# Broadcast rows in one transfer, two gates one scan later, one write a slot earlier, in a Mamba and attention kernel

## The chip, the cores and the metric

The kernel runs on one core of a Trainium2 chip. The metric is the device time of one execution in microseconds (us). Before the change it is 8030.78 us, the median of three runs (8016.75 to 8032.62).

## The reference, cut to what matters

The input `x` is 4 images of 512 channels and 64 x 64 = 4096 positions. Layer 0 normalises it, cuts the 512 channels into 4 chunks of 128, and runs a Mamba block on each chunk; layer 1 is a linear attention with 8 heads. Both add to `x`. The change lies in the Mamba block, whose core is a scan over the positions with 16 states for each of 256 inner channels:

```python
def step(h, inp):
    dt_t, B_t, C_t, x_t = inp
    dA = jnp.exp(dt_t[:, :, None] * A)
    h = dA * h + (dt_t * x_t)[:, :, None] * B_t[:, None, :]
    y = jnp.einsum('bds,bs->bd', h, C_t)
    return (h, y)
...
y = ys.transpose(1, 0, 2) + xc * D_param
y = y * jax.nn.silu(z)                      # the gate
return jnp.einsum('bld,od->blo', y, out_proj_w)
```

`B_t` and `C_t` have one value for each position and state and are the same for all channels; `dt_t` and `u = dt_t * x_t` have one for each position and channel and are the same for all states.

## The kernel before

**Steps.** A step is one image, one tile of 512 positions and one chunk: 4 x 8 x 4 = 128 steps. A step has 256 channels x 16 states of scans over 512 positions. The 128 partitions hold 32 channels x 4 states at a time, so a scan instruction does 128 of the 4096 rows and a step has 32 scans. They are dealt to 16 slots of two scans. Slots 0 to 7 belong to the first 128 channels (e = 0), slots 8 to 15 to the second (e = 1). Two slots are a group: one set of 4 states (`q`), four scans, one tile `h` of 128 x 4 x 512. `h` has two buffers.

**What a group needs.** `dA` (ACT, L715) is the exponential of `dt` spread over the states; `bx` (POOL, L722, `drive`) is `u` times `B`, three slots ahead of its scan. VectorE does the scans (L775). After the group, VectorE multiplies three quarters of `h` with `C` from PSUM (L798, `product`, called behind the first scan of the next group), POOL the last quarter with `C` from SBUF (L790), and TensorE folds the states into `y` (`fold_states`). When a half is through, VectorE multiplies `y` with the silu of `z` (L818, `gate`), and `out_proj` uses that at slot 4 for the step before.

**The broadcast data.** All of it goes through DRAM and comes back spread over the partitions, issued by SyncE (SP in the profile):

- `b_all`, 128 x 512 for each group: 4 rows of `b_rows`, each to 32 partitions. `c_sb`, 128 x 128: the same for the last quarter of `c_rows`. `for_states` (L687) does either with four transfers, one per state. `c_tail` and `b_row` call it in every odd slot: `c_sb` for the group that starts next, `b_all` for a group three further on. `c_sb` has two buffers and `b_all` three.
- `d_all`: for each half, `dt` (v = 0) and then `u` (v = 1), spread over the states by four transfers of 256 KB each (`spread`, L633). The half e = 1 is spread in slots 0 and 1 of its own step, the half e = 0 of the next step in slots 7 and 9. `d_all` has two buffers. A first `drive` on the half e = 1 is issued in slot 5.
- `d_rows`: `dt` of the next step is written to DRAM in slot 4 and `u` in slot 8 (`to_rows`, L624). `u` is made by POOL in slot 6 (L631, `times_input`), in place over `dt`.

**Order.** The order of every engine's instructions is the order in which the code issues them: `slot` (L759) and the function `after` (L1146) that it calls at its end. SP issues one transfer after the other and waits at each for what that one needs: a free buffer, written rows, and one of eight completion semaphores that the program deals out in turn to SP's transfers, so that a transfer also waits until the one eight before it has landed.

Of the kernel before, what the change touches and what calls it, by code (L numbers as in the profile page):

```python
# [24 lines left out]
def kernel(  # L25
# [24 lines left out]
    nc = tc.nc  # L50
# [4 lines left out]
    NH = DI // P  # L55
# [3 lines left out]
    BLK = 32  # L59
    KS = P // BLK  # L60
# [563 lines left out]
    def to_rows(f, v, nm):  # L624

        d_rows = dram.tile([P, NH, T], F32, tag=f"d_rows{v}", name=f"d_rows{v}_{nm}")
        f["d_rows", v] = d_rows
        nc.sync.dma_start(d_rows, f["dt"])
# [43 lines left out]
    JJ = NJ // 2  # L672
    SLOTS = NH * NQ * JJ
    AWAY = (3, 10)

    def place(g):

        n, r = divmod(g, SLOTS)
        e, r = divmod(r, NQ * JJ)
        return n, e, *divmod(r, JJ)  # L680
# [5 lines left out]

    def for_states(dst, rows_, q):  # L687

        for k in range(KS):
            nc.sync.dma_start(  # L690
                dst[k * BLK : (k + 1) * BLK, :], rows_[q * KS + k, :].partition_broadcast(BLK)
            )

    def b_row(g):
        n, e, q, _ = place(g)
# [37 lines left out]
    def carry_over(g):  # L733

        n, e, _, _ = place(g)
        nc.gpsimd.tensor_tensor(
            carry[:, e], a_t[:, e],
            fs[n]["d_all", e][:, 0, :, 0].unsqueeze(2).to_broadcast([P, NJ, NQ]), ALU.mult,
        )
# [11 lines left out]
    def starts_half(g, last):  # L751

        return g < last and g % (SLOTS // NH) == 0 and steps[g // SLOTS][1] > 0

    def keep(g, h, copy):
        n, e, q, _ = place(g)
        copy(st[:, steps[n][2], e, q, :], h[:, :, T - 1])  # L757

    def slot(g, last, after):  # L759
        n, e, q, jj = place(g)  # L760
        if starts_half(g + DRIVE + 1, last):
            carry_over(g + DRIVE + 1)
        if g + DRIVE < last:
            drive(g + DRIVE)
        if jj == 0:
            hs[g // JJ] = wk.tile([P, NJ, T], F32, tag="h", name=f"h_{g}", bufs=2)
        else:
            if g + 1 < last:
                c_tail(g + 1)
            if g + 1 + 3 * JJ < last:  # L770
                b_row(g + 1 + 3 * JJ)
        h = hs[g // JJ]
        for i in range(2):
            j = jj * 2 + i
            nc.vector.tensor_tensor_scan(  # L775
                h[:, j, :], dAs.pop(2 * g + i), bx[:, g % RING, i, :], 0.0, ALU.mult, ALU.add,
            )
            if i == 1 and jj == JJ - 1 and g % SLOTS - 1 not in AWAY:
                keep(g, h, nc.scalar.copy)
            if 2 * g + i + LEAD < 2 * last:  # L780
                decay(2 * g + i + LEAD)
            if i == 0 and jj == 0 and g:
                product(g - 1)
                fold_states(g - 1, last)
        if starts_half(g + DRIVE, last):
            carry_decay(g + DRIVE)
        if jj == JJ - 1:
            if g % SLOTS - 1 in AWAY:
                keep(g, h, nc.gpsimd.tensor_copy)
            nc.gpsimd.tensor_tensor(  # L790
                h[:, :, CUT:], h[:, :, CUT:], bc(c_sb.pop(g // JJ), NJ), ALU.mult
            )
        after()

    def product(g):

        own = hs[g // JJ][:, :, :CUT]
        nc.vector.tensor_tensor(own, own, bc(c_all.pop(g // JJ), NJ), ALU.mult)  # L798
# [17 lines left out]
    def gate(f, n, e):  # L816
        z = f["xz"][:, 1, e, :]
        nc.vector.tensor_tensor(z, ys.pop((n, e)), z, ALU.mult)  # L818
# [224 lines left out]
    names = [f"{b}_{t}_{c}" for b, t, c in steps]  # L1043
    fs = [{} for _ in steps]
# [87 lines left out]
    with tc.manual_schedule():  # L1132
        credit, seen, mix, held[0], held_x[0] = 0.0, work["mm"], iter(()), 0, 0
        for n, (b, t, c) in enumerate(steps):
            f, nm = fs[n], names[n]
            before = fs[n - 1] if n else None
            nxt = fs[n + 1] if n + 1 < N else None
            front = step_inputs(n + 2) if n + 2 < N else iter(())
            last_mix, mix = mix, mixers(fs[n + 2], names[n + 2]) if n + 2 < N else iter(())
            if c == 0 and (t + 1 < NT or b + 1 < B):  # L1140
                add_to(ahead, tile_norm(b, t + 1) if t + 1 < NT else tile_norm(b + 1, 0))
            if c == 0 and t == 0 and b + 1 < B:
                add_to(light, input_norm(b + 1))
            assert c != 2 or not ahead
            for s in range(SLOTS):
                def after():  # L1146
                    nonlocal credit, seen
                    now[0] = n * SLOTS + s
                    for what in [w for at, w in due if at <= now[0]]:
                        what()  # L1150
                    due[:] = [d for d in due if d[0] > now[0]]
                    if s < 2:
                        next(last_mix, None)
                    if s in (0, 1):
                        spread(f, 1, s, nm)
                    if s == 1 and before is not None:
                        gate(before, n - 1, 1)
                    if s == 2 and nxt is not None:
                        time_banks(nxt, names[n + 1])
                    if s == 3 and nxt is not None:  # L1160
                        nc.scalar.preload_act_table_set("softplus")
                        time_steps(nxt, names[n + 1])
                        nc.scalar.preload_act_table_set("natural_log_exp_and_others")
                    if s == 6 and before is not None:
                        pb_, pt_, pc_ = steps[n - 1]
                        with_skip(before, xn[pb_, pt_], pc_)
                        if pc_ == NC - 1:
                            add_to(late, leave(pb_, pt_))
                    if s in (3, 5, 6, 7, 8, 9):
                        next(front, None)  # L1170
                    if s in (4, 8) and nxt is not None:
                        to_rows(nxt, int(s == 8), names[n + 1])
                    if s == 6 and nxt is not None:
                        times_input(nxt)
                    if s == 4 and before is not None:
                        pb_, pt_, pc_ = steps[n - 1]
                        out_proj(before, xn[pb_, pt_], pc_, names[n - 1])
                    if s in (7, 9) and nxt is not None:
                        spread(nxt, 0, int(s == 9), names[n + 1])
                    if s == 9:  # L1180
                        gate(f, n, 0)
                    if s == 10 and n + 2 < N:
                        silu(n + 2)
                        nc.scalar.preload_act_table_set("natural_log_exp_and_others")
                    if s >= 12:
                        next(mix, None)
                    may = [
                        what for k, what in ((0, "wide"), (1, "one ahead"), (2, "two ahead"))
                        if any(a - 2 * k <= s <= a - k for a in AWAY) or (k == 2 and s == SLOTS - 1)
                    ]  # L1190
                    if light and light[0][1] == "wait" or s in AWAY and not any(
                        q and q[0][1] == "wide" for q in (ahead, late)
                    ):
                        one(light)

                    limit[0] = 1 if 0 < s < 6 else 2
                    credit = min(credit + 3.5 - (work["mm"] - seen), 2.6)
                    busy = False
                    for queue in (ahead, late, rest):
                        kind = queue[0][1] if queue else None  # L1200
                        if queue is ahead or kind == "free" or credit > 0 or kind == "more" and not busy:
                            start = work["mm"]
                            one(queue, ANYWHERE if queue is ahead and (c, s) > (1, 4) else may)
                            credit -= work["mm"] - start
                            busy = busy or work["mm"] - start > 1
                    seen = work["mm"]

                slot(n * SLOTS + s, N * SLOTS, after)
            fs[n - 1].clear() if n else None
        product(N * SLOTS - 1)  # L1210
        fold_states(N * SLOTS - 1, N * SLOTS)
        now[0] = None
        for _, what in due:
            what()
# [59 lines left out]
```

## Time and profile before

| what | value |
|---|---|
| median of the runs | 8030.78 us |
| profiled execution, its own time | 8041.96 us |
| its span | 8040.3 us |
| mean granted TensorE clock | 0.891 |
| first to last `dA` (all 128 steps) | 118.0 to 7562.9 us |
| in 118 to 7563 us: VectorE busy | 6855.94 us |
| in 118 to 7563 us: POOL busy | 6681.71 us |
| in 118 to 7563 us: TensorE busy | 6005.43 us |
| in 118 to 7563 us: ACT busy | 5367.02 us |
| in 118 to 7563 us: mean busy share of the 16 DMA engines | 0.66 |
| transfers issued by SP | 11064, of which 4096 `b_all` and 4096 `c_sb` |

The busy times are those of one profiled execution. Idle time of an engine is put down to what ended it; where a wait has several semaphores, to the one that came last, and a semaphore that several transfers share in turn can carry the name of another one.

### The profile page before, as it was taken

The page shows a single profiled execution, that of the slowest core. Times are in us where ns is not written, and L with a number is a line of the kernel's source. Part 1 is how long each engine was busy: PE and PEld are TensorE (multiplying, and loading weights), DVE is VectorE, ACT ScalarE, POOL GpSimd, SP SyncE. Part 2 cuts the span into 40 slices and gives each one's busy share as a digit, 9 for nine tenths or more (in the row PEclk, how much of TensorE's full clock was granted, in tenths as well). Part 3 has the DMA queues.
Part 4 walks back from the last instruction along what each step waited for, and adds up shares of the span by engine and source line. Part 5 has one row for each costly group of instructions (what it writes and reads, how often), then busy time and mean ns, then how long its engine had stood idle before and what let it go on. Part 6 is the DMA issues. An engine that isn't in the chain of part 4 may idle for free.

```text
span 8040.3 us, 92566 instructions
## 1 busy us (share of the span) xinstructions
PE 6500.2 (81%) x24880; PEld 2130.3 (26%) x24880; DVE 6925.7 (86%) x6022; ACT 5501.7 (68%) x9185; POOL 6691.3 (83%) x4789
## 2 busy tenths in 40 slices
PE   5677777677788888888788888888778888888599
PEld 1111211121223222322222222322122232322144
DVE  5999999999999899989999999998989999988600
ACT  4667777777777777677777777777777777777421
POOL 3999999999898899889888889888989898888600
PEclk7788888888899999999899999999799999999699
DMA  5666666666666666676666666676666666677402
GB/s 151 165 166 161 153 150 159 156 158 160 168 163 169 149 165 158 172 189 170 167 159 171 171 153 162 157 183 186 160 156 160 157 159 155 155 187 183 113 32 89
DMA packets 829200, 1266.00 MB, mean 157 GB/s; under 512 B 183912, under 2 KB 317560, under 8 KB 816384
## 3 DMA queue, kind: packets, MB, share of 16 engines
q1 hardware_dynamic: 804736, 1222.32, 59.7%
q0 software_dynamic: 16896, 33.56, 2.4%
q10 hardware_dynamic: 7040, 4.20, 0.2%
q8 instruction: 195, 3.19, 0.2%
q14 instruction: 333, 2.73, 0.1%
HBM read 1052.78 MB, written 206.57 MB: 157 GB/s over the span
## 4 chain that ended last, share of the span: by engine, by line
DVE 35%; PE 25%; ACT 14%; DMA 10%; POOL 6%; issue 6%; SPq 4%; POOLq 0%; DVEq 0%; ACTq 0%
DVE h L775 21%; DVE h L798 10%; PE pq L124 5%; PE pc L124 5%; PE y L124 4%; ACT dA L715 4%; POOL bx L722 4%; DMA d_all<-d_rows 3%; SPq L690 3%; DMA c_sb<-c_rows 3%; PE pr L124 2%; PE po L124 2%; ACT xz L1083 2%; PE pp L124 2%; DMA xn<-in_x_dram 2%
## 5 line engine op out<-in xcount | busy, mean ns | idle before, releaser
L722 POOL TENSOR_TENSOR bx<-d_all,b_all 128x1024 f32<-128x1024 f32 x2048 | 4861.7, 2376 | 404.5 <-DMA c_sb<-c_rows 162.4
L775 DVE TENSOR_TENSOR_SCAN h<-dA,bx 128x512 f32<-128x512 f32 x4096 | 4753.6, 1206 | 502.8 <-ACT dA L715 236.5
L715 ACT ACTIVATE dA<-d_all,a_t 128x512 f32<-128x512 f32 x4096 | 2778.5, 686 | 1445.5 <-DVE h L775 1382.9
L798 DVE TENSOR_TENSOR h<-h,c_all 128x1536 f32<-128x1536 f32 x1024 | 1769.5, 1728 | 0.1
L790 POOL TENSOR_TENSOR h<-h,c_sb 128x512 f32<-128x512 f32 x1024 | 1317.2, 1286 | 237.2 <-ACT st L757 130.4
L124 PE MATMUL y<-h,fold 128*32 128x512 f32 x8192 | 1281.1, 702 | 138.0 <-POOL h L790 132.7
L124 PE MATMUL c_all<-parts,sel 128*128 128x384 bf16 x1024 | 369.5, 361 | 1125.8 <-DVE h L798 1123.4
L124 PE MATMUL pc<-xn,w_cv 128*128 128x512 f32 x2048 | 1042.0, 643 | 98.5 <-DVE xn L414 48.4
L124 PE MATMUL pq<-w_qk,xa 128*128 128x512 f32 x2048 | 965.8, 605 | 1.6 <-ACT xa L367 1.6
L124 PEld LDWEIGHTS <-sel 128*128 128x128 bf16 x1280 | 126.7, 99 | 1763.9 <-DVE h L798 1546.1
L124 PEld LDWEIGHTS pc<-xn,w_cv 128*128 128x128 f32 x2048 | 388.5, 200 | 721.1 <-issue 426.3
L124 PEld LDWEIGHTS pq<-w_qk,xa 128*128 128x128 f32 x2048 | 398.4, 196 | 435.2 <-issue 418.0
L124 PE MATMUL pr<-xb,m 128*128 128x512 f32 x1024 | 485.7, 613 | 4.1 <-ACT res L1014 3.2
L124 PE MATMUL pp<-xn,w_pr 128*128 128x512 f32 x1024 | 478.9, 598 | 4.8 <-DVE xn L414 4.8
L124 PEld LDWEIGHTS y<-h,fold 128*32 128x32 f32 x8192 | 171.0, 114 | 715.2 <-issue 340.8
L124 PE MATMUL y<-xz,dg 32*32 32x512 f32 x2048 | 338.7, 737 | 0.0
L124 PE MATMUL pd<-xz,w_xp 128*128 128x512 f32 x512 | 325.5, 769 | 7.8 <-ACT xz L1083 7.8
L631 POOL TENSOR_TENSOR dt<-dt,xz 128x1024 f32<-128x1024 f32 x128 | 302.0, 2360 | 31.8 <-DMA d_rows<-dt 27.5
L867 ACT ACTIVATE kq<-pq 128x512 f32<-128x512 f32 x256 | 150.6, 588 | 258.2 <-PE pq L124 257.0
L757 ACT COPY st<-h 128x4 f32<-128x4 f32 x896 | 172.4, 192 | 204.0 <-DVE h L775 201.0
L124 PE MATMUL pz<-xn,w_z 128*128 128x512 f32 x512 | 294.6, 671 | 5.4 <-ACT xz L608 5.2
L874 DVE TENSOR_TENSOR kq<-pk,kq 128x256 f32<-128x256 f32 x124 | 50.7, 409 | 250.9 <-PE pk L124 250.9
(182 smaller groups left out, 6200.0 us busy)
## 6 DMA issues: line engine op xcount, KB each, us to landing
d_all<-d_rows SPq DMA_DIRECT2D x2048, 256.0 KB, 5.1
b_all<-b_rows SPq DMA_DIRECT2D x4096, 64.0 KB, 2.2
d_rows<-dt SPq DMA_DIRECT2D x256, 512.0 KB, 6.2
c_sb<-c_rows SPq DMA_DIRECT2D x4096, 16.0 KB, 4.4
xs<-in_x_dram SPq DMA_DIRECT2D x32, 1024.0 KB, 6.7
xn<-in_x_dram SPq DMA_DIRECT2D x32, 1024.0 KB, 8.5
xr<-in_x_dram POOLq DMA_DIRECT2D x32, 1024.0 KB, 10.8
x<-xr SPq DMA_DIRECT2D x32, 1024.0 KB, 4.1
```

What stands on the lines that cost most here:

```text
L124: nc.tensor.matmul(out_, lhsT, rhs, **how)
L631: nc.gpsimd.tensor_tensor(f["dt"], f["dt"], f["xz"][:, 0], ALU.mult)
L690: nc.sync.dma_start(dst[k * BLK : (k + 1) * BLK, :], rows_[q * KS + k, :].partition_broadcast(BLK))
L715: nc.scalar.activation(dAs[k], fs[n]["d_all", e][:, 0, j, :], AF.Exp, scale=a_t[:, e, j, q : q + 1])
L722: nc.gpsimd.tensor_tensor(bx[:, g % RING], fs[n]["d_all", e][:, 1, jj * 2 : jj * 2 + 2, :], bc(b_all[g // JJ], 2), ALU.mult,)
L757: copy(st[:, steps[n][2], e, q, :], h[:, :, T - 1])
L775: nc.vector.tensor_tensor_scan(h[:, j, :], dAs.pop(2 * g + i), bx[:, g % RING, i, :], 0.0, ALU.mult, ALU.add,)
L790: nc.gpsimd.tensor_tensor(h[:, :, CUT:], h[:, :, CUT:], bc(c_sb.pop(g // JJ), NJ), ALU.mult)
L798: nc.vector.tensor_tensor(own, own, bc(c_all.pop(g // JJ), NJ), ALU.mult)
L867: nc.scalar.activation(qk[i], pq, AF.Relu)
L874: nc.vector.tensor_tensor(kq, pk, kq, ALU.add)
L1083: nc.scalar.activation(fs[n]["xz"], fs[n]["xz"], AF.Silu)
```

## The change

`for_states` issues one transfer instead of four: the source is walked as 4 rows x 32 repeats x the row, the destination as 128 partitions. The two gates move from the end of slots 1 and 9 to behind the first scan of slots 2 and 10, ahead of `product`. `u` is written out at slot 7 instead of 8, ahead of the `spread` of that slot.

```diff
     def for_states(dst, rows_, q):
-        for k in range(KS):
-            nc.sync.dma_start(
-                dst[k * BLK : (k + 1) * BLK, :], rows_[q * KS + k, :].partition_broadcast(BLK)
-            )
+        src = rows_[q * KS : (q + 1) * KS, :].unsqueeze(1).to_broadcast([KS, BLK, dst.shape[-1]])
+        nc.sync.dma_start(dst, src)
...
             if i == 0 and jj == 0 and g:
+                if g % SLOTS == JJ and n:
+                    gate(fs[n - 1], n - 1, 1)
+                if g % SLOTS == SLOTS // NH + JJ:
+                    gate(fs[n], n, 0)
                 product(g - 1)
                 fold_states(g - 1, last)
...
-                    if s == 1 and before is not None:
-                        gate(before, n - 1, 1)
...
-                    if s in (4, 8) and nxt is not None:
-                        to_rows(nxt, int(s == 8), names[n + 1])
+                    if s in (4, 7) and nxt is not None:
+                        to_rows(nxt, int(s == 7), names[n + 1])
...
-                    if s == 9:
-                        gate(f, n, 0)
```

## Prediction

> **What bounds the kernel now.** I read the engines' busy time, the waits of POOL, VectorE and SP, one step in the timeline, and then the DMA lines.
>
> ```profile
> PE 6500.2 (81%) x24880; PEld 2130.3 (26%) x24880; DVE 6925.7 (86%) x6022; ACT 5501.7 (68%) x9185; POOL 6691.3 (83%) x4789
> ```
>
> The 128 steps run from 118 to 7563 us, 58.2 us each (3.64 per slot). In that stretch VectorE is busy 92% and POOL 90%: two engines bound it together, and only their idle time can be won.
>
> ```profile
> DVE h L775 <- ACT dA L715: 236.5, 210, 3.9
> DVE h L775 <- PE y L124: 73.5, 81, 3.0
> DVE xz L818 <- PE y L124: 69.7, 82, 4.4
> DVE h L775 <- POOL bx L731: 58.0, 63, 5.3
> DVE h L775 <- POOL bx L722: 55.6, 12, 46.6
> ...
> POOL bx L722 <- DMA c_sb<-c_rows: 162.4, 115, 4.2
> POOL h L790 <- ACT st L757: 130.4, 104, 5.5
> POOL bx L722 <- DVE h L775: 91.1, 90, 4.0
> POOL bx L722 <- DMA b_all<-b_rows: 73.9, 48, 4.3
> ...
> SPq L690 <- DMA d_all<-d_rows: 1108.5, 1355, 3.4
> ```
>
> Columns: total us, times, longest. `bx` does not read `c_sb`: 115 waits in 128 steps are one per step, and the timeline shows which.
>
> ```profile
> 3982.15 1.75 SPq L690 DMA_DIRECT2D c_sb<-c_rows  x4
> 3984.01 2.59 SPq L690 DMA_DIRECT2D b_all<-b_rows  x4
> 3986.69 2.64 SPq L639 DMA_DIRECT2D d_all<-d_rows  x4
> 3989.80 3.17 SPq L690 DMA_DIRECT2D c_sb<-c_rows  x4
> 3994.33 3.67 SPq L690 DMA_DIRECT2D b_all<-b_rows  x4
> 3998.05 1.84 SPq L639 DMA_DIRECT2D d_all<-d_rows  x4
> ...
> 3999.84 2.36 POOL L722 TENSOR_TENSOR bx<-d_all,b_all 128x1024 f32<-128x1024 f32 x1
> 4005.90 2.36 POOL L722 TENSOR_TENSOR bx<-d_all,b_all 128x1024 f32<-128x1024 f32 x1 [3.70 <-DMA c_sb<-c_rows]
> ```
>
> This is slots 15, 0 and 1 on SP. The last POOL line is the first `drive` of the half e = 1: it waits for the `u` part of `d_all`, which SP could issue only at 3998.05, 8.25 us after the `c_sb` of slot 1, because each of the eight transfers before it waited for the one eight ahead to land. So SP's issue and its eight semaphores make POOL late. All POOL waits on DMA in the steps come to 348.7 us: `bx` 162.4 + 73.9 + 18.1 + 16.6 + 8.2, L790 47.0 + 16.8 + 5.7. VectorE's waits laid to POOL, straight or through `y`, are 73.5 + 69.7 + 58.0 + 9.0 (55.6 less one of 46.6 at the start) = 210.2. POOL's idle time before L722 and L790 is 404.5 + 237.2, so one us of POOL's idle time costs VectorE 210.2/641.7 = 0.33 us; were the DMA waits alone to blame, 0.6. I take 0.33.
>
> **One transfer for four rows: SP.** A step has 32 `b_all` and 32 `c_sb` transfers of 0.365 and 0.419 us (medians of the tile views), 25.1 us of SP's 58.2; 8 of each remain, 6.3 us, or 9.5 at the 0.595 us of the longest-issuing SP transfers (L295). Eight semaphores then reach back across two slots, not one.
>
> **The same: DMA engines.** What may be lost lies here. Every SP transfer of before ran on 16 engines: q1's 804736 packets are 627712 data rows plus 16 for each of 11064 transfers.
>
> ```profile
> q1 hardware_dynamic: 804736, 1222.32, 59.7%
> q0 software_dynamic: 16896, 33.56, 2.4%
> q10 hardware_dynamic: 7040, 4.20, 0.2%
> ```
>
> On q10 the rows of ACT's 27 transfers make 6680, and the other 360 are 21 x 16 + 2 x 8 + 4 x 2, where two transfers have 8 rows (`w_dt`) and four have 2 (`b_qk`). So the number of engines went with the outer count. The changed source walks 4 rows outermost against 128 partitions: the bounds are 16 engines and 4. I take 4, the row of the 2- and 8-row transfers being nearest.
>
> The Trainium skill speaks against this change: "DMA: Bandwidth & Descriptors", "Why a DMA increments its semaphore by 16 and not by 1", says the largest number up to 16 that divides the outer counts of both sides is used, here 4, and its "Rules for kernel authors" warn of a small outer dimension. By the rule the sum is the four-engine one; without it, the 16-engine rival.
>
> Mean packet times from the trace's packet records: `b_all` 119 ns, `d_all` 149, `c_sb` 34 (most 25 to 27), `d_rows` 176, `w_o` and `w_v` 91 (32 packets in a row per engine from DRAM, as one `b_all` would be on four). Per step an engine carries now: `b_all` 64 x 0.119 = 7.6, `c_sb` 64 x 0.034 = 2.2, `d_all` 128 x 0.149 = 19.1, `d_rows` 16 x 0.176 = 2.8, loads and stores of tiles 6.0 (a quarter of a tile's: 64 packets of `xs` and `xn` at 0.103, 32 of `xr` at 0.189, 32 of the output at 0.09, 24 of 8 KB at 0.36), receipts 1.0: 38.7 us. The page's 62.1% x 8040/128 is 39.0, so the terms are whole.
>
> After, on the four engines: `b_all` 256 x 0.091 = 23.3, `c_sb` 256 x 0.027 = 6.9, `d_all` 128 x 0.110 = 14.1 (between 0.091 and 0.149: while four engines lag, they carry their rows without the other twelve), `d_rows` 2.8, tiles 6.0, receipts 0.5: 53.6 us, 92% of a step. Bounds: 0.084 for `b_all` (its fastest packets) and 0.091 for `d_all` give 49.3 (85%); 0.091, 0.034 and 0.149 give 60.4 (104%); 0.119 for `b_all` as well gives 67.6 (116%). In my value they do not saturate, but they are near it.
>
> **Where the stall goes.** The step above, on four engines: from 3982.15 two `c_sb` (0.9 each), two `b_all` (2.9), two `d_all` (32 packets at 0.110, 3.5) make 14.6; 1.1 from issue to first packet (`b_all`, median) and 0.9 from last packet to landing (`w_v`) make 16.6. Landed at 3998.8, wanted at 3999.84 + 2.36 = 4002.2: no wait. This step also has POOL's `xr` load, 32 x 0.189 = 6.0: landed at 4004.8, a wait of 2.6 where the trace has 3.7. An `xr` comes in one step of four, so 0.65 us per step where 162.4/128 = 1.27 are lost: 79 us of POOL won. The other 186 us of POOL's DMA waits come from SP being late with `b_all` and `c_sb`, whose buffers are free some four slots ahead; I take three quarters as gone, 140. So 219 x 0.33 = 72 us.
>
> **The gates.** Nothing, by my reading. The gate waits for the last `y` of a half; the first scan of slot 2 (or 10) writes the `h` buffer which those same matmuls read, so the 69.7 us pass from L818 to that scan. `product` and all that PE queues behind it come after both in either order; `out_proj` is two slots off. Bounds: -69.7 if the scan needed no such wait; +17 if a tenth of the 256 scans wait for something else (some 420 of 4096 do) and no longer have the 0.67 us gate as cover.
>
> **`u` a slot earlier.** SP meets L631 (2.36 us on POOL) sooner, with a 512 KB write, four `d_all` and slot 9's `c_sb` queued behind. `d_all` e = 0 is first wanted in slot 12, `c_sb` two slots later: nothing, covered by 3.64 us per slot. Bounds: +100 (2.36 x 128 x 0.33) without cover; -26 if all waits laid to `d_rows` and `d_all` on L722 (8.2 + 18.1) go.
>
> **Sum.** 8041.96 - 72 = 7970 by the profiled execution; it is 11.2 above the median, so 7959, said as 7960.
>
> **Rivals.**
> - *Sixteen engines after all* (the transfer is cut by its 128 partitions): `b_all` and `c_sb` stay at 9.8 us per engine and SP's relief remains. All 348.7 us go: at 0.33 to 0.6, 7821 to 7916, about 7890. For it: SP's own rows. Against it: q10's count.
> - *It evens out*: four-engine landings eat what SP saves. 8031.
> - *Slower: `d_all` behind `b_all` on four engines.* Place: the spread of slot 1, whose last quarter waits behind a `b_all` that now fills four engines for 2.9 to 3.8 us. With 0.119 and 0.149 the sum of the step above is 21.3, 1.3 late, and 7.3 with `xr`: 2.8 us per step for 1.27 now (with rounding, 1.4 to 1.5 more), some 180 us of POOL, 60 to 108 in time: 8090 to 8138, about 8110. It decides when `d_all` needs over some 0.14 us per packet on those engines.
> - *Slower still: the four engines become the bound*, if their load passes 58.2 us: 60.4 gives 2.2 x 128 = 282 more (8313), 67.6 gives 9.4 x 128 (9234). For it: `b_all` packets at 0.119 today.
>
> **How the numbers follow.** Forecast 0.40, sixteen engines 0.10, evens out 0.07, `d_all` late 0.27, four engines the bound 0.16. A measurement can tell some 0.2% (16 us) from no change. Faster 0.50, same 0.07, slower 0.43. The range from 7860 to 8320 leaves out most of the bound case and the lower part of the sixteen-engine one, under 0.2. The forecast's own range is 7900 to 8010.
>
> **What would show it.** q1's packets: 627712 data rows plus 16 for each of 4920 transfers if all engines take part; 24576 fewer (2048 transfers x 12) if four do. SP's waits on `d_all` fall far below 1108 us. `b_all` lands in 5 to 8 us for 2.2 per quarter. POOL's `bx` waits on DMA fall under 100 us if I am right and rise over 350 if `d_all` is late; a mean DMA share unchanged near 0.66 with rising POOL waits means four saturated engines. VectorE's wait at L818 vanishes and comes back at L775 on PE `y`. I am wrong if POOL's DMA waits fall and the time does not.

## The result, and the profile after

The changed kernel takes 8543.49 us (median of four runs, 8535.69 to 8555.13) against 8025.4 us for the kernel before, run beside it: a ratio of 1.0647, 95% interval [1.0629, 1.0666]. It is slower by 6.5%, and lies above the upper end of the range. The case that came true is the one given a chance of 0.16, "the four engines become the bound"; with 60.4 us per step it had 8313.

The first lines of the profile of the changed kernel, which took 8543.74 us by its own time with a span of 8542.0 us:

```profile
PE 6635.7 (78%) x24835; PEld 2160.7 (25%) x24880; DVE 6937.3 (81%) x6022; ACT 5504.3 (64%) x9185; POOL 6673.5 (78%) x4789
q1 hardware_dynamic: 681856, 1221.82, 57.8%
```

The work of VectorE and POOL is what it was (11.6 us more, 17.8 less); the 501.8 us by which the profiled execution is longer are idle time of these two. q1's count is to the packet the one that the prediction gave for four engines (627712 + 16 x 4920 - 12 x 2048 = 681856).

The waits of POOL and VectorE (total us, times, longest):

```profile
POOL bx L720 <- DMA d_all<-d_rows: 450.3, 175, 8.8
DVE h L773 <- POOL bx L729: 394.9, 198, 6.6
DVE h L773 <- ACT dA L713: 355.4, 224, 9.8
POOL h L792 <- DMA c_sb<-c_rows: 262.0, 79, 9.2
DVE h L773 <- PE y L124: 169.0, 121, 5.9
POOL bx L720 <- DMA b_all<-b_rows: 29.3, 21, 5.3
```

POOL's waits on DMA in the steps come to 777.2 us (450.3 + 262.0 + 29.3 and three of 10.8 to 13.9), where there were 348.7. VectorE's wait on `bx` is 336.9 longer, that on `y` 95.5, that on `dA` 118.9, and the one at the gate is 67.6 shorter (69.7 became 2.1): 483.7 of the 501.8. The name behind POOL's largest wait has become `d_all`, which the change does not touch.

The waits of SP in the changed kernel:

```profile
SPq L690 <- POOL bx L729: 1152.2, 680, 5.9
SPq L690 <- POOL h L792: 747.5, 475, 8.8
...
SPq L690 <- DMA d_all<-d_rows: 281.0, 371, 1.8
```

1108.5 us of standing behind `d_all` have become 281.0, and SP's largest waits are now for buffers that POOL frees (all its waits on engines went from 1415 to 4137 us). It is not rid of the landings: its waits on DMA, whatever name they carry, come to 1695 us where they were 1594. But the transfers that POOL stands behind start early and land late, as the timeline shows in slots 9 to 13 of one step, for the half e = 0 of the next (start, length, engine, count):

```profile
4229.27 0.51 SPq L690 DMA_DIRECT2D b_all<-b_rows  x1
4229.87 2.29 SPq L639 DMA_DIRECT2D d_all<-d_rows  x4
...
4233.12 0.53 SPq L690 DMA_DIRECT2D c_sb<-c_rows  x1
...
4245.40 2.35 POOL L720 TENSOR_TENSOR bx<-d_all,b_all 128x1024 f32<-128x1024 f32 x1 [3.61 <-DMA d_all<-d_rows]
```

The four `d_all` transfers of the `u` part are issued almost without a pause, by 4232.16, and POOL still waits for them at 4245.4: 13.2 us after the last issue. The prediction took this half as covered by its slots. In the whole run the first `bx` of the half e = 0 waits 171.3 us for DMA, where it waited 29.7, and the first `bx` of the half e = 1 waits 314.5 for 227.4 (both from the second step on).

Where they stay is in the trace's semaphore records. Each `d_all` transfer has 16 updates from its engines. For the last of the four above, issued at 4231.86, twelve come by 4237.30 and the other four between 4242.27 and 4245.24; POOL starts at 4245.40. Over all 2048 `d_all` transfers the last update comes 5.5 us after the twelfth (median), where it was 0.26 us before: twelve engines are done early and four are behind.

What the engines do in that time is in the packet records, by the number of packets in flight at once on the 16 engines (for a packet's price: at its start, between 0.2 and 8.0 ms):

| | before | after |
|---|---|---|
| none in flight, share of the span | 16.5% | 5.9% |
| 4 or 5 in flight | 5% | 39.6% |
| mean of a 2 KB packet of q1 | 133.8 ns | 138.6 ns |
| of a 2 KB packet of q1 with 16 or more in flight | 139.4 ns | 156.9 ns |
| of a 2 KB packet of q1 with 5 or 6 in flight | 124.9 ns | 98.8 ns |
| mean of a 512 B packet | 33.7 ns | 38.2 ns |

In the steps the moments without any packet come to under 1%. For two fifths of the time only four or five packets are in flight, and for 3.1% of the time fewer than four (between 0.4 and 7.4 ms). With the late four updates of each `d_all` transfer this reads as four engines that work almost without a pause while the other twelve stand idle, and the step has their length, 62.0 us (first to last `bx`, 126.4 to 8066.1, over 128) where it was 58.1.

### The profile page after: what moved, and what is told of

It is laid out like the page before. It is cut to its first block, busy times and chain, and to the rows that moved or that the text cites. A ratio compares the mean times of both kernels' runs of the same rounds, so it can differ in the third digit from the quotient of the medians.

```text
span 8542.0 us, 83399 instructions
## 1 busy us (share of the span) xinstructions
PE 6635.7 (78%) x24835; PEld 2160.7 (25%) x24880; DVE 6937.3 (81%) x6022; ACT 5504.3 (64%) x9185; POOL 6673.5 (78%) x4789
## 3 DMA queue, kind: packets, MB, share of 16 engines
q1 hardware_dynamic: 681856, 1221.82, 57.8%
## 5 line engine op out<-in xcount | busy, mean ns | idle before, releaser
L720 POOL TENSOR_TENSOR bx<-d_all,b_all 128x1024 f32<-128x1024 f32 x2048 | 4861.8, 2377 | 684.5 <-DMA d_all<-d_rows 450.3
L124 PE MATMUL y<-h,fold 128*32 128x512 f32 x8192 | 1319.8, 722 | 478.2 <-POOL h L792 459.4
L792 POOL TENSOR_TENSOR h<-h,c_sb 128x512 f32<-128x512 f32 x1024 | 1318.5, 1288 | 467.5 <-DMA c_sb<-c_rows 262.0
L124 PE MATMUL pc<-xn,w_cv 128*128 128x512 f32 x2048 | 1072.6, 659 | 102.2 <-DVE xn L414 48.2
L124 PE MATMUL po<-xz,w_op 128*128 128x512 f32 x512 | 267.6, 646 | 3.3 <-DVE xz L820 3.3
```

What stands on the lines that cost most here:

```text
L124: nc.tensor.matmul(out_, lhsT, rhs, **how)
L720: nc.gpsimd.tensor_tensor(bx[:, g % RING], fs[n]["d_all", e][:, 1, jj * 2 : jj * 2 + 2, :], bc(b_all[g // JJ], 2), ALU.mult,)
L792: nc.gpsimd.tensor_tensor(h[:, :, CUT:], h[:, :, CUT:], bc(c_sb.pop(g // JJ), NJ), ALU.mult)
```

## The experiments

The theory was that the four engines' load sets the step. Its rivals: the other two edits do the harm; one large transfer is slow in itself, on whatever engines (rival 3 of the expectations); and, later, not the load but the long transfer does it, by holding up the queue behind it and SP's eight semaphores. Where an expectation has letters for theories, they are its own.

**The parts alone.** `rows_only` has only the edit of `for_states`, `gates_u` only the other two.

> Only the transfers of four rows in one; gates and the write of u as before. Theory 1 (the four engines that carry b_all and c_sb are the bound): nearly all of the loss is here, 8520 to 8560 us, q1 681856 packets. Rival 2 (the moved gates or the write of u in slot 7 cost the time, by SP or VectorE waiting in order): at most 8150 us.

> Only the gates and the write of u moved; four transfers per group as before. Theory 1: 8010 to 8035 us, no change that can be told, and VectorE's 69.7 us wait for y passes from the gate to the scan ahead of it. Rival 2: 8300 us or more.

Measured: `rows_only` 8565.82 us, 1.0659 [1.0644, 1.0673], q1 again 681856, POOL's `bx` behind `d_all` 496.6 us. `gates_u` 8068.88 us, 1.0043 [1.0030, 1.0055]. The whole loss is in the one transfer; the other edits cost 0.4%, more than `gates_u` had been expected to (it lies outside its 8010 to 8035), and next to the saturated engines not even that.

**The same transfer on more engines.** If the number of rows walked outermost sets the number of engines, holding each row several times in DRAM widens it. `copies2` and `copies4` are the changed kernel with `b_rows` and `c_rows` stored two and four times:

```diff
-        src = rows_[q * KS : (q + 1) * KS, :].unsqueeze(1).to_broadcast([KS, BLK, dst.shape[-1]])
+        src = rows_[q * KS : (q + 1) * KS].rearrange("k r t -> (k r) t").unsqueeze(1)
+        src = src.to_broadcast([KS * COPIES, BLK // COPIES, dst.shape[-1]])
         nc.sync.dma_start(dst, src)
...
-            nc.sync.dma_start(b_rows, dtr[RANK : RANK + NST, :])
+            b_src = dtr[RANK : RANK + NST, :].unsqueeze(1).to_broadcast([NST, COPIES, T])
+            nc.sync.dma_start(b_rows, b_src)
```

(`c_rows` likewise.)

> The whole change, but b_rows and c_rows are written twice over, so that the source walks 8 rows with 16 repeats each. If the engines used go with the outer count, 8 take part and q1 loses 2048 x 8 = 16384 receipts against 16 per transfer. Theory 1: the load of the busiest engine falls from about 62 us per step to about 47, less than a step, and the time is 7930 to 8050 us. Rival 3 (one large transfer is slow in itself: longer to issue, later to land, whatever engines carry it): 8400 to 8550 us, as the change.

> As copies2 with four copies: 16 rows outermost, 8 repeats, so all 16 engines by the outer count and no receipts missing. Theory 1: load about 39 us per step on every engine, POOL's waits on DMA under 100 us, 7880 to 7990 us, faster than before. Rival 3: 8400 to 8550 us.

Measured: `copies2` 8077.0 us, 1.0051 [1.0037, 1.0064], q1 694144; `copies4` 8021.93 us, 0.9983 [0.9974, 0.9992], q1 718720. Both counts are those of 8 and of 16 engines: 681856 + 2048 x 4 and + 2048 x 12, with 4096 and 12288 rows for the stored copies. SP issues the same transfers in all three; the number of engines brings the 6.5% back, and a transfer of four rows is not slow in itself. POOL's wait on `d_all` goes from 450.3 over 146.3 to 29.6 us. Both are slower than the theory had them (7930 to 8050 and 7880 to 7990): the gain that was to come on top of the loss regained did not show, and the next runs look for it.

**What the good part is worth, and each small edit.** `copies4_only` is `copies4` with gates and `u` as before; `gates_only` and `u_only` have one of the small edits each.

> Four copies of the rows in DRAM and one transfer on 16 engines, gates and write of u as before. If the moved gates and write cost what they cost beside four transfers per group (0.43%), this gains 0.5 to 0.7% on before, 7985 to 8005 us, with POOL's waits on DMA again under 60 us. Rival: once POOL no longer waits on DMA the moves cost nothing, and this is equal to the kernel with all three, 8015 to 8030 us.

> Only the two gates moved behind the first scan. Theory A (the write of u ahead of four d_all transfers cost the 0.43% of the two moves): 8030 to 8050 us, as before. Theory B (the gates cost it: 0.67 us of VectorE now stand between the first scan and the product, and the scans of slot 2 and 10 meet POOL and ACT later): 8060 to 8075 us.

> Only the write of u at slot 7. Theory A: 8060 to 8075 us, with POOL waiting longer on d_all or SP longer on L631. Theory B: 8030 to 8050 us.

Measured: `copies4_only` 7990.63 us, 0.9928 [0.9916, 0.9941], faster than both kernels. `gates_only` 8067.8 us, 1.0029 [1.0019, 1.0040]. `u_only` 8054.03 us, 1.0011 [1.0002, 1.0020]. So the moves still cost what they cost beside four transfers, and it is the gates that cost most of it; `u_only` lies between the ranges of its two theories.

POOL's waits in `copies4_only`:

```profile
POOL h L792 <- ACT st L759: 278.1, 213, 5.8
POOL bx L724 <- DVE h L777: 169.8, 163, 6.8
...
POOL bx L724 <- DMA d_all<-d_rows: 22.5, 18, 2.7
```

The DMA waits are all but gone (60.7 us in the steps), and POOL now waits for ACT and VectorE: 278.1 + 169.8 where these two lines had 130.4 + 91.1. Of 288 us won at the DMA, 226 are given back there at once.

In `gates_only` VectorE's waits show where the 0.3% lies:

```profile
DVE h L775 <- POOL bx L731: 132.5, 81, 4.9
DVE h L775 <- PE y L124: 105.4, 99, 4.6
```

The wait at the gate is gone (2.1 us left) and the scan's wait for `y` grew by 31.9, so the two together fell by 35.7; but the scan's wait for `bx` rose from 58.0 to 132.5, which more than eats it. Fit for a gate that no longer fills the time before the first scan of a half; that it is this is argued, not shown by a run.

**Which of the two broadcasts.** `b_one` sends only `b_all` in one transfer, `c_one` only `c_sb`; the rest is as before:

```diff
+        if dst.shape[-1] == T:
+            src = rows_[q * KS : (q + 1) * KS, :].unsqueeze(1).to_broadcast([KS, BLK, dst.shape[-1]])
+            nc.sync.dma_start(dst, src)
+            return
         for k in range(KS):
             ...
```

(`c_one` has `!= T`.)

> Only b_all in one transfer of four rows; c_sb stays in four, gates and u as before. By packet times of the changed kernel the load of the four engines is about 56 us per step (25 of them b_all), just under the 58.2 of a step. If the load of the four engines decides: 8060 to 8250 us, well under the 8566 us of both in one transfer. If one long transfer is late by itself, most of the 6.6% stays: 8400 us or more.

> The kernel before with one edit: c_sb's four rows go in one transfer, b_all stays in four. Theory A (the load of the four engines sets the step): those engines carry per step b_all 64 packets x 0.119 = 7.6, c_sb 256 x 0.038 = 9.7, d_all 128 x 0.15 = 19.2, d_rows 2.8, tiles 6.0, receipts 0.8, together 46 us of a step of 58: no bound, time within 0.4% of before (8010 to 8070). Theory B (any long transfer on four engines holds up the queue behind it, however small the load): c_sb's landing rises for all of its eight transfers a step and d_all waits behind them, so a good part of the loss is there: 8150 to 8400.

Measured: `b_one` 8536.27 us, 1.0607 [1.0593, 1.0622], which misses its expectation of 8060 to 8250 by far; `c_one` 7989.01 us, 0.9925 [0.9908, 0.9942], faster by more than expected and level with `copies4_only`. The short transfers on four engines are a gain, the long ones bring nearly all the loss. POOL's waits on DMA in `c_one`, the two largest:

```profile
POOL bx L726 <- DMA b_all<-b_rows: 44.6, 38, 3.6
POOL bx L726 <- DMA d_rows<-dt: 40.9, 23, 2.3
```

With those after them (20.4, 18.6, 18.2, 12.9, 9.4) they make 165 us for 348.7. But `b_one` opened a question. By the terms (the 64.4 us of the next section, less 192 rows of `c_sb` at 0.038) its four engines have some 57 us of work a step, and its step is 61.9 us; and SP there stands behind the landing of `b_all`:

```profile
SPq L694 <- DMA b_all<-b_rows: 1188.5, 515, 8.6
```

So it might be the long transfer with SP's eight semaphores, and not the load.

**Load against long transfer.** `b4x4` keeps four `b_all` transfers of 64 KB, but has each on four engines; `two_two` doubles the load of an engine by sending two rows at a time.

```diff
 b4x4 (b_rows stored four times)
+            d_, r_ = dst[k * BLK : (k + 1) * BLK, :], rows_[q * KS + k]
+            if dst.shape[-1] == T:
+                nc.sync.dma_start(d_, r_.unsqueeze(1).to_broadcast([COPIES, BLK // COPIES, T]))
 two_two
+        for k in range(0, KS, 2):
+            src = rows_[q * KS + k : q * KS + k + 2, :].unsqueeze(1)
+            src = src.to_broadcast([2, BLK, dst.shape[-1]])
+            nc.sync.dma_start(dst[k * BLK : (k + 2) * BLK, :], src)
```

> The kernel before with one edit: b_rows holds each row four times in DRAM, and each of b_all's four transfers a group walks those four copies outermost and repeats each for 8 partitions. It stays four transfers of 64 KB with 16 x 4 fewer receipts, but on four engines: the four engines carry the same bytes as in b_one, and no transfer is longer than 8 packets an engine. q1 then has 804736 - 4096 x 12 = 755584 packets (4096 b_all transfers), and a few for the stored copies. Theory A (load of the four engines): 8500 to 8580, as b_one. Theory B (the one long transfer, with SP's eight semaphores and d_all behind it, makes the loss): most of it goes, 8050 to 8200.

> The kernel before with one edit: the four rows go in two transfers of two rows each, so that two engines carry each. Theory A (load): if it is always the same two engines, they carry per step b_all 512 packets x 0.09 to 0.12 = 46 to 61, c_sb 512 x 0.027 to 0.038 = 14 to 19, d_all 128 x 0.11 to 0.15 = 14 to 19, d_rows 2.8, tiles 6.0: 83 to 108 us a step, which makes 11.2 to 14.4 ms with the 590 us outside of the steps. Theory B (the long transfer and its place in the queue): a transfer has 32 packets an engine as in the changed kernel, there are twice as many, and the time is near the changed kernel's, 8500 to 9000.

Measured: `b4x4` 8683.61 us, 1.0789 [1.0773, 1.0805]; `two_two` 11728.76 us, 1.4576 [1.4548, 1.4604]. From the page and SP's waits of `b4x4`, the page of `two_two`, and the largest waits of POOL in `two_two`:

```profile
q1 hardware_dynamic: 761728, 1234.70, 55.1%
...
SPq L694 <- DMA d_all<-d_rows: 1004.5, 1560, 2.7
```

```profile
q1 hardware_dynamic: 681856, 1221.82, 41.1%
...
DMA 66%; PE 9%; POOL 8%; SPq 7%; DVE 4%; issue 3%; ACT 2%; POOLq 0%; ACTq 0%; DVEq 0%
```

```profile
POOL bx L722 <- DMA d_all<-d_rows: 1378.8, 197, 24.6
POOL bx L722 <- DMA b_all<-b_rows: 971.0, 388, 8.1
```

`b4x4` has no long transfer, SP issues four `b_all` for each one of `b_one`, and the loss is there, larger than load had it (8500 to 8580): a long transfer is not what is needed for it. (Its count is 804736 - 4096 x 12 + 6144 rows for the copies: four engines.) But load alone is not the whole account of these two kernels. Fewer than four packets are in flight for 7.5% of the time in `b_one` and for 18.2% in `b4x4`, against 3.1% in the changed kernel (all between 0.4 and 7.4 ms), so there the four engines are not always busy, and SP stands 1188.5 us behind `b_all` in the one and 1004.5 us behind `d_all` in the other (1108.5 before). That SP's waits for late landings make up the rest is possible; no run separates it. In `two_two` the second line is the chain of work that ended last: DMA is two thirds of it. Exactly two packets are in flight for 49.1% of the span, and in the steps there is no moment without one. The step is 87.0 us (136.3 to 11267.7, over 128), within the 83 to 108 that load predicts; the queue theory had 8500 to 9000 us. q1's mean share of the DMA engines falls to 41.1% while DMA is the bound.

The steps side by side, first to last `bx` over 128, with the engines that each broadcast ran on:

| kernel | `b_all` | `c_sb` | step, us |
|---|---|---|---|
| before | 16 | 16 | 58.1 |
| `copies4_only` | 16 | 16 | 57.7 |
| `c_one` | 16 | 4 | 57.8 |
| `copies2` (gates and `u` moved) | 8 | 8 | 58.5 |
| `b_one` | 4 | 16 | 61.9 |
| the changed kernel | 4 | 4 | 62.0 |
| `b4x4` | 4 | 16 | 63.2 |
| `two_two` | 2 | 2 | 87.0 |

## Why the prediction was wrong

- **Where it failed: the price of the rows that the four engines carry, "`d_all` 128 x 0.110 = 14.1", taken because "while four engines lag, they carry their rows without the other twelve".** They do lag, by 5.5 us. But the twelve have `d_all` rows of their own, and those come at a time when the four, which hardly pause, carry something too: in the stretch shown, their late rows of the `dt` part beside the twelve's `u`, and then their `u` beside the twelve's `xs`. A sum that has all of `b_all` at 0.091 and nearly all of `d_all` at the price without company leaves that out. The counts show how much it is. Of the 2 KB packets between 0.2 and 8.0 ms, 136477 start with 11 or fewer in flight. The four carry some 193000 rows of `b_all` and `d_all` in that time (131072 + 65536 in all 128 steps), so at least some 57000 of them, 110 of the 384 of an engine and step, are carried with 12 or more in flight; with 16 or more a packet takes 156.9 ns. As an estimate with a third at that price, whichever rows they are: 256 x 0.099 + 128 x 0.157 = 25.3 + 20.1 = 45.4 us, for 23.3 + 14.1 = 37.4. The records do not name the engine of a packet, so this is worked out from counts.
- **The other term was low too, by less.** `c_sb` 256 x 0.038 = 9.7 for 6.9. With 2.8, 6.0 and 0.5 the sum is 64.4; measured are 62.0. The value taken was 53.6, and the bounds 49.3 to 67.6 held it: 60.4 was one step away, with 0.149 for `d_all` and 0.034 for `c_sb`, the rows of before. I left measured rows for an argument, and the result hung on that: by the prediction's own terms it is a gain below 58.2 and the bound above, where each further us costs 128.
- **The chances.** Load between 49.3 and 67.6 has its middle at 58.5; 0.16 for passing 58.2 was too little for that.
- **The four engines themselves: right.** 4, 8, 16 and 2 rows outermost give by q1's counts 4, 8, 16 and 2 engines. The Trainium skill states it as the rule that the prediction weighed ("DMA: Bandwidth & Descriptors", "Why a DMA increments its semaphore by 16 and not by 1"); every count here agrees with it, and with what its "Rules for kernel authors" say of a small outer dimension: it confines the whole transfer to that many engines at most. Whether that costs time went with how much was sent that way: for `b_all` it did, for `c_sb` alone, a quarter of the bytes, it did not, and `c_one` is faster than before.
- **SP's relief and its price: right where the engines have room.** `c_one` takes 184 us off POOL's DMA waits and 61 us off the time (8050.37 to 7989.01): 0.33, the factor that was taken. `copies4_only` takes off 288 us and brings 54 to 58 us: 0.2. The last hundred are worth nothing, since POOL then meets ACT and VectorE. So the "72 us" for 219 were about 60, and the sixteen-engine rival's 115 to 210 us for 348.7 were too much: it measured 0.7% (58 us), and 0.2% in the full change.
- **The rival "`d_all` behind `b_all`"** had the mechanism that the waits show, `bx` behind `d_all`. It priced one landing in an otherwise unloaded row; at its own place, the half e = 1, it had 2.8 us per step, and measured are 2.5 (314.5 over 127). What it left out is the half e = 0, late as well, and the price in time: POOL's waits on DMA grew by 428.5 us and the time by 502, where 0.33 to 0.6 of them were taken. With the four engines hardly ever idle the lateness does not end with the slot.
- **Gates: wrong sign, small.** "Nothing" was 0.3% (23 us by its ratio), just beyond the bound of +17. The wait passed from the gate to the scan as said, but 74.5 us of waits on `bx` came with it.
- **`u`: nothing, nearly.** 1.0011, some 9 us, within -26 to +100.
- **The signs.** q1's count, SP's wait on `d_all` and the gate's wait came as written. POOL's `bx` waits on DMA rose over 350 (493.5). `b_all` lands 10.9 us after its issue (median, by its last semaphore update), not in 5 to 8. The mean DMA share, "unchanged near 0.66", is 0.63 in the steps: near enough, with rising waits of POOL, to the sign of four saturated engines.

Left open: why `b_one` is as slow as the full change, though its four engines carry 192 rows of `c_sb` less a step, 7 us by the terms. The 7.5% of the time with fewer than four packets in flight are part of it, with SP behind the landing of `b_all`. 2 KB packets are also 6.3 ns longer there (144.9 against 138.6 on average), which would make up most of it if all of that fell on the four engines; and the records can't show on which it fell. Nor was it tried why `c_sb` on four engines adds almost nothing once `b_all` is there.

## What to carry to other kernels

Before merging transfers, count on how many engines the merged one runs, and add up per step what those engines alone carry, with everything else that passes through them: the mean DMA share hides it, and falls as the few engines become the bound. Where the sum comes near the step, take the slower measured packet time for a good part of their rows (here a third), since the other engines' own rows come at some time while the few are busy, and give the saturated case the weight that the bounds give it. Merge the short transfers, which here took the issuing engine's waits away at no cost while the four engines had room, and for the long ones first make the outer count large (four copies of a row in DRAM cost 120 KB of writes a step here), then merge.

## What the runs showed of the hardware that was not expected

- When four engines fall behind, the others run ahead of them within the same transfer: the last of the 16 semaphore updates of a `d_all` transfer comes 5.5 us after the twelfth in the changed kernel, 0.34 in `c_one` and 0.43 in `copies4_only` (medians).
- A transfer with four rows outermost is not slow by itself: 0.51 us to issue (`b_all`, median) against 0.365 for one of the four, and, for the short `c_sb`, as good for the kernel as 16 engines (`c_one` 57.8 us a step, `copies4_only` 57.7).
- With two engines saturated the issue itself takes long: the median issue of `b_all` in `two_two` is 1.28 us and the longest 7.65, where the shortest is 0.48. No run shows why.
- The granted TensorE clock is lower the slower the kernel is: 0.896 in `c_one`, 0.872 in `b4x4`, 0.781 in `two_two`. TensorE's busy time rises with it (6463.9, 6690.3 and 7453.1 us for the same matmuls), which makes it look busier than its work is.
